# Attention scores as float32r products of split halves, and exponentials of three score tiles at a time

## The chip, the cores and the metric

The kernel runs on one core of one Trainium2 chip (trn2). The metric is the device time of one execution in microseconds. Before the change it is 12858.68 us, the median of three runs (12857.75 to 12866.36).

TensorE is called PE (its weight loads PEld), VectorE DVE, ScalarE ACT, GpSimd POOL. SP is the sync engine, which here only issues DMAs. Every engine takes its own instructions in the order in which the program gives them.

## The reference

The program is one layer of a state-space convolution on 4 images of 64 x 64 tokens with 128 channels, then one layer of attention with a mixture of experts. Only the attention's core is touched. Cut to that:

```python
def _qz_ring(phi):
    c = jnp.cos(phi)
    P = jnp.cumprod(c, axis=-1)
    z0 = jnp.prod(c[..., 1:], axis=-1, keepdims=True)
    return jnp.concatenate([z0, P[..., 1:]], axis=-1)
...
heads = x.reshape(Bs, Ss, H, D)          # 4 images, 4096 tokens, 16 heads of 8
qkv = _qz_ring(heads + rx_theta)
q = jnp.transpose(qkv, (0, 2, 1, 3))
scores = jnp.einsum('bhsd,bhtd->bhst', q, q) / np.sqrt(D)
attn = jax.nn.softmax(scores, axis=-1)
ctx = jnp.einsum('bhst,bhtd->bhsd', attn, q)
```

Queries, keys and values are the same array. For each image and head there are 4096 x 4096 scores, each a sum over only 8 channels. All data are float32.

## The kernel before, in words

**Stages.** A first stage (up to about 2150 us) makes the inputs of the convolution's scans for all images and runs the scans of image 0. Then `opening(0)` (called at line 1470) prepares attention for image 0: `tokens` (line 778) forms the normalised tokens, `heads` and `rings` (lines 867 and 877) form the queries. Then `loop` (line 903) runs once for each of the four images. The calls `beside(i)` (lines 1484 to 1498, and the lambda at 1525) put other work between the rounds of attention: in the loops of images 0 to 2 the scans of the next image (`following`) and, once these are through, the next image's `opening`; also the part `after` attention of the image before (`last`). In the last loop, which runs `by_block`, there are only the parts after attention and the search and gathering of the experts. A closing stage of some 250 us follows. The order on each engine is the order of these calls: the schedule is manual, and `Pace.run(share)` advances a part by `share` of a step for each call.

**Scans.** `Scans.of_image` (line 484) works in 384 steps for an image. One step has an exponential on ACT over 128x1024 (line 530), a product, a scan and a product on DVE (lines 537, 546, 551). In two of every four steps, eight products on PE (line 578) add up the states into `y`.

**Queries and values to memory.** `rings` works on 512 tokens (eight pieces for an image). It forms `ring`, copies it into `v_g` with a one beside each head's 8 values (so that the value product also gives the softmax's denominator), transposes 32x32 blocks (line 893), and SP stores the transposed queries to `d_q` in 16 DMAs (line 899). POOL stores `v_g` to `d_v`.

**The loop.** It loads all queries of the image (`qT`, channels by tokens) and all values (`v`) in 16 DMAs (lines 913 and 914). A turn is one `j` of 4 (the heads 4k + j, k = 0 to 3) and one block of 512 queries. `masked` (line 921) makes a copy of the query block in which only the channels of the heads 4k + j are not zero, so that 32 rows of `qT` times 32 rows of the masked block give the scores of exactly one head. A round is a turn and 128 keys (`kc`, 32 of them); there are 32 x 32 = 1024 rounds in a loop.

- `scores(i)` (line 926): four products of 32 rows, 128 keys by 512 queries, one for each k, into two PSUM tiles of two banks; ACT takes the exponential of each tile (line 939, 128x1024) into SBUF. There are three such PSUM tiles.
- `values(i)` (line 942): four products of 128 keys, 32 columns by 512 queries, that add up in the four 32-partition strips of one PSUM bank, `acc`.
- PE's order is scores(0), scores(1), values(0), scores(2), values(1) and so on, with what `beside` puts behind each `values`.
- At a turn's end `sums` (line 954) copies `acc` on ACT (line 957), and POOL stores the result three rounds later.

PSUM has eight banks: six for scores, one for `acc`, one for all other work.

The profile counts a float32 product as two weight loads and two matmul records.

Of the kernel before, what the change touches and what calls it, by code (L numbers as in the profile page):

```python
# [11 lines left out]
F32 = mybir.dt.float32  # L12
AF = mybir.ActivationFunctionType
ALU = mybir.AluOpType
PSUM = bass.MemoryType.PSUM

P = 128
# [11 lines left out]
B_ROW, C_ROW, X_ROWS = 8, 40, 104  # L29
H, D, FFN = 16, 8, 512  # L30
VW = 9
VPAD = 168
QB = 512
TWO_PI_HI = 6.28125
TWO_PI_LO = 2.0 * math.pi - TWO_PI_HI
ROUND = 1.5 * 2.0**23
# [641 lines left out]
class Attention:  # L678
# [3 lines left out]
    def __init__(self, tc, ctx, w, gate, cols, ident, bank, dram, t1, w_out, sums, sz, x):  # L682
# [20 lines left out]
        self.w1 = const.tile([D, FFN], F32, name="w1")  # L703
        self.w2 = const.tile([P, 4, C], F32, name="w2")

        self.mask = const.tile([P, 4], F32, name="mask")
        self.gate = const.tile([P, E], F32, name="gate")
        self.gate_b = const.tile([2 * E, 1], F32, name="gate_b")
        for k in range(2):
# [1 line left out]
        with tc.tile_pool(name="a_load", bufs=1) as load, tc.tile_pool(  # L711
            name="a_load_ps", bufs=2, space=PSUM
        ) as load_ps:
            raw = load.tile([P, C], F32, name="raw_comb")
            nc.sync.dma_start(out=raw, in_=w["w_comb"])
            ps = load_ps.tile([P, 512], F32, tag="ps", name="ps_comb")
            nc.tensor.transpose(ps[:, :C], raw, ident)
            nc.vector.tensor_copy(self.w_comb, ps[:, :C])
            raw = load.tile([P, 4, D], F32, name="raw_w1")
            nc.sync.dma_start(out=raw, in_=w["w1"].rearrange("(f p) d -> p f d", p=P))  # L720
            ps = load_ps.tile([P, 512], F32, tag="ps", name="ps_w1")
            for f in range(4):
                nc.tensor.transpose(ps[:D, f * P : (f + 1) * P], raw[:, f, :], ident)
            nc.vector.tensor_copy(self.w1, ps[:D])
            raw = load.tile([P, FFN], F32, name="raw_w2")
            nc.sync.dma_start(out=raw, in_=w["w2"])
            ps = load_ps.tile([P, 512], F32, tag="ps", name="ps_w2")
            for f in range(4):
                nc.tensor.transpose(ps[:, f * P : (f + 1) * P], raw[:, f * P : (f + 1) * P], ident)
            nc.vector.tensor_copy(self.w2.rearrange("p f c -> p (f c)"), ps)  # L730
            raw = load.tile([4, 4, 4, D], F32, name="raw_mask")
            nc.gpsimd.memset(raw, 0.0)
            nc.gpsimd.affine_select(
                out=raw, in_=raw, compare_op=ALU.not_equal, fill=1.0,
                base=0, pattern=[[0, 4], [-1, 4], [0, D]], channel_multiplier=1,
            )
            ps = load_ps.tile([P, 512], F32, tag="ps", name="ps_mask")
            nc.tensor.transpose(ps[:, :4], raw.rearrange("j i k d -> j (i k d)"), ident[:4, :4])
            nc.vector.tensor_copy(self.mask, ps[:, :4])
            raw = load.tile([E, C], F32, name="raw_gate")  # L740
            nc.scalar.dma_start(out=raw, in_=gate_w)
            ps = load_ps.tile([P, 512], F32, tag="ps", name="ps_gate")
            nc.tensor.transpose(ps[:, :E], raw, ident[:E, :E])
            nc.vector.tensor_copy(self.gate, ps[:, :E])
# [6 lines left out]
    def begin(self, loop):  # L751

        tc = self.tc
        self.pieces_of(loop, 2)
        self.big = loop.enter_context(tc.tile_pool(name="a_big", bufs=1))
        self.mid = loop.enter_context(tc.tile_pool(name="a_mid", bufs=2))
        self.exps = loop.enter_context(tc.tile_pool(name="a_exps", bufs=4))
        self.ps_s = loop.enter_context(tc.tile_pool(name="a_ps_s", bufs=3, space=PSUM))
        self.ps_o = loop.enter_context(tc.tile_pool(name="a_ps_o", bufs=1, space=PSUM))

    def pieces_of(self, ctx, n, ahead=2, opening=True):
# [4 lines left out]

        self.values = []
        for i in range(2 if opening else 0):
            v_g = self.one.tile([P, 4, VPAD], F32, tag=f"v_g{i}", name=f"v_g{n}_{i}")
            nc.gpsimd.memset(v_g[:, :, H * VW :], 0.0)  # L770
            heads = v_g[:, :, : H * VW].rearrange("p t (h e) -> p t h e", e=VW)
            nc.gpsimd.memset(heads[:, :, :, D], 1.0)
            self.values.append((v_g, heads[:, :, :, :D]))

    def piece(self, shape, tag, name):
        return self.one.tile(shape, F32, tag=tag, bufs=self.n, name=name)
# [74 lines left out]
    def opening(self, b):  # L851
# [1 line left out]


        self.u[b] = self.dram.tile([P, NT, C], F32, name=f"d_un_{b}")
        self.v[b] = self.dram.tile([P, NT, VPAD], F32, name=f"d_v_{b}")
        self.q[b] = self.dram.tile([P, L], F32, name=f"d_q_{b}")
        self.angled[b] = 0
        angles, parts = [], []
        for half in range(2):  # L860
# [16 lines left out]
    def rings(self, b, g, a):  # L877
# [8 lines left out]
            nc.vector.tensor_mul(ring[:, :, d], ring[:, :, d - 1], a[:, :, d])  # L886
        copy(ring[:, :, 0], ring[:, :, D - 1])
        nc.vector.tensor_mul(ring[:, :, 1:], ring[:, :, 1:], a[:, :, 0:1].to_broadcast([P, 4 * H, D - 1]))
        copy(values, ring.rearrange("p (t h) d -> p t h d", h=H))
        nc.gpsimd.dma_start(out=self.v[b][:, cut, :], in_=v_g)  # L890

        blocks = a.rearrange("p (t h) d -> p t (h d)", h=H)
        nc.vector.transpose(blocks.rearrange("p t c -> p (t c)"), ring.rearrange("p h d -> p (h d)"))
        yield
        to = self.q[b][:, g * 512 : (g + 1) * 512].rearrange("(k r) (t i c) -> i k r t c", r=32, i=4, c=32)
        for i in range(4):
            rows = blocks[32 * i : 32 * i + 32].rearrange("r t (k c) -> k r t c", c=32)
            for k in range(4):
                nc.sync.dma_start(out=to[i, k], in_=rows[k])
            if i % 2:  # L900
                yield

    def loop(self, b, beside, by_block=False):
# [3 lines left out]
        self.context[b] = self.dram.tile([P, L], F32, name=f"d_ctx_{b}")  # L907
        self.total[b] = self.dram.tile([L // QB, H, QB], F32, name=f"d_sum_{b}")
        self.whole[b] = 0
        qT = self.big.tile([P, L], F32, tag="qT", name=f"qT_{b}")  # L910
        v = self.big.tile([P, NT, VPAD], F32, tag="v", name=f"v_{b}")
        for g in range(NT // 4):
            nc.sync.dma_start(out=qT[:, g * 512 : (g + 1) * 512], in_=self.q[b][:, g * 512 : (g + 1) * 512])
            nc.sync.dma_start(out=v[:, g * 4 : g * 4 + 4, :], in_=self.v[b][:, g * 4 : g * 4 + 4, :])
        turns = [(j, qb) for j in range(4) for qb in range(L // QB)]
        if by_block:
            turns.sort(key=lambda turn: turn[1])
        rounds = [(j, qb, kc) for j, qb in turns for kc in range(NT)]
        queries, es, accs, later = {}, {}, {}, {}

        def masked(j, qb):
            t = self.mid.tile([P, QB], F32, tag="qm", name=f"qm_{b}_{j}_{qb}")
            nc.vector.tensor_scalar_mul(t, qT[:, qb * QB : (qb + 1) * QB], self.mask[:, j : j + 1])
            queries[j, qb] = t

        def scores(i):

            j, qb, kc = rounds[i]
            es[i] = []
            for pair in range(2):  # L930
                s_ps = self.ps_s.tile([P, 2, QB], F32, tag="s", name=f"s_{b}_{i}_{pair}")
                for k in range(2):
                    at = 32 * (2 * pair + k)
                    nc.tensor.matmul(  # L934
                        s_ps[:, k, :], qT[at : at + 32, kc * P : (kc + 1) * P], queries[j, qb][at : at + 32, :],
                        start=True, stop=True,
                    )
                e = self.exps.tile([P, 2, QB], F32, tag="e", name=f"e_{b}_{i}_{pair}")
                nc.scalar.activation(e, s_ps, AF.Exp, scale=1.0 / math.sqrt(D))  # L939
                es[i].append(e)  # L940

        def values(i):
            j, qb, kc = rounds[i]
            if kc == 0:
                accs[j, qb] = self.ps_o.tile([P, QB], F32, tag="acc", name=f"acc_{b}_{j}_{qb}")
            for k in range(4):
                h = 4 * k + j
                nc.tensor.matmul(  # L948
                    accs[j, qb][32 * k : 32 * k + 32, :], v[:, kc, h * VW : h * VW + 32],
                    es[i][k // 2][:, k % 2, :], start=(kc == 0), stop=(kc == NT - 1),  # L950
                )
            del es[i]

        def sums(j, qb, i):
# [14 lines left out]
                if by_block and j == 3:  # L969
                    self.whole[b] = qb + 1  # L970

            later[i + 3] = store

        masked(0, 0)
        scores(0)
        for i, (j, qb, kc) in enumerate(rounds):
            if i + 1 < len(rounds):
                scores(i + 1)
            values(i)
            if kc == NT - 1:  # L980
                sums(j, qb, i)
            if kc == NT - 12 and i + 12 < len(rounds):
                masked(*rounds[i + 12][:2])
            if i in later:
                later.pop(i)()
            beside(i)
# [443 lines left out]
def tile_kernel(tc, ctx, x, in_proj_w, dirs, out_proj_w, attn, gate, weight1, weight2, out):  # L1430
# [47 lines left out]
    with tc.manual_schedule():  # L1478
        last = Pace()
        n = 3 * NC * NB  # L1480
        for b in range(nb - 1):
            opens = Pace(block.opening(b + 1))

            def beside(i):
# [1 line left out]
                left = 2.1 * (n + 1 - scans.steps.get(b + 1, 0))  # L1486
                block.lag = 2 if left > 0.0 else 0
                scans.did.clear()
                following.run(min(1.3, max(0.5, left / max(1, 860 - i))))
                other = last if not last.done else opens if left == 0.0 else None  # L1490
                if other is None:
                    return
# [22 lines left out]
    with tc.manual_schedule():  # L1515
# [6 lines left out]
            block.after(nb - 1, range(0, 4)), block.after(nb - 1, range(4, 6)), block.after(nb - 1, range(6, blocks - 1)),  # L1522
            experts.search(pairs[-1], blocks - 1),
        )
        block.loop(nb - 1, lambda i: last.run(0.92), True)
        last.rest()
    loop.close()
    with ExitStack() as end:
# [48 lines left out]
```

## Time and profile before

| | |
|---|---|
| median of the runs | 12858.68 us |
| span of the profiled execution, first to last instruction | 12857.0 us (the lowest run is 12857.75) |
| busy: PE, ACT, DVE, POOL | 94%, 84%, 68%, 24% |
| first exponential of the loops of images 0, 1, 2, 3 | 2430, 4982, 7566, 10130 us |
| last exponential of the last loop | 12607.6 us |
| mean granted TensorE clock | 0.964 |

The span in 40 equal slices of 321 us; each digit is the busy share in tenths, PEclk the granted clock of TensorE:

```profile
PE   7888887599999999999999999999999999999996
PEld 3333333122222222333332222332332223333323
DVE  7999998788888777988888779888884211101112
ACT  5677766599999988999999889999998888888882
POOL 2324342232323222223232222332331000000000
PEclk8898988799999999999999999999999999999997
DMA  5666666555555455554554555545553100000005
```

The loops begin in slice 8. From there PE is at nine tenths throughout; ACT is there too until the last scan ends, in slice 31, where DVE falls to almost nothing. The chain of work that ended last lies on PE for 84% of the span, and its lines are these:

```profile
PE s L934 38%; PE acc L948 31%; PE y L578 5%; PE cv L386 3%; PE sp L444 2%; DVE h L546 2%; PE fo L1093 1%; ACT e L939 1%; PE xd L400 1%; PE h L1082 1%; DMA w<-in_L_ffn_weight_dram 1%; DVE dB L537 0%; ACT e L432 0%; ACT ln L437 0%; ACT s L434 0%
```

In the profile's groups of instructions the first number after the bar is the time in which at least one of the group ran, the second the mean duration of one in nanoseconds; then the idle time just ahead of them and what ended it. Matmuls overlap, so the mean duration of one says little about how many fit in a microsecond; the distance from start to start does.

Waits of SP, the DMA queue's own (total in us, times, longest), the largest three and one more that the prediction uses:

```profile
SPq L516 <- PE y L578: 2937.9, 350, 24.7
SPq L567 <- DMA d_du<-x_delta: 2096.1, 236, 23.6
SPq L516 <- DVE h L546: 1306.8, 283, 14.3
...
SPq L1063 <- DMA d_xn<-x1r: 651.5, 8, 103.3
```

### The profile page before, as it was taken

The numbers are of one execution on the slowest core, as the hardware profiler recorded it, in microseconds if no ns is written. First come the engines' busy times: TensorE is split into PE (matmuls) and PEld (weight loads), VectorE is DVE, ScalarE is ACT, GpSimd is POOL, SyncE is SP. The second block draws the span as 40 slices with busy tenths as digits, with TensorE's granted clock in tenths as the row PEclk, the third lists the DMA queues.
The fourth block names the chain that finished last, engine by engine and source line by source line (L and its number), as shares of the span: only waits on it lengthen the run. The fifth ranks groups of instructions, "written<-read, shape, count | busy, mean of one in ns | idle before, by whom it ended". The sixth has DMA issues, their size and how long they took to land.

```text
span 12857.0 us, 215633 instructions
## 1 busy us (share of the span) xinstructions
PE 12118.4 (94%) x85447; PEld 3884.6 (30%) x85447; DVE 8712.2 (68%) x8866; ACT 10742.2 (84%) x10860; POOL 3043.0 (24%) x4007
## 2 busy tenths in 40 slices
PE   7888887599999999999999999999999999999996
PEld 3333333122222222333332222332332223333323
DVE  7999998788888777988888779888884211101112
ACT  5677766599999988999999889999998888888882
POOL 2324342232323222223232222332331000000000
PEclk8898988799999999999999999999999999999997
DMA  5666666555555455554554555545553100000005
GB/s 162 198 188 183 188 183 189 148 134 138 138 135 137 122 147 144 143 130 123 130 134 123 146 140 146 133 121 129 133 122 99 51 18 13 22 17 22 13 21 171
DMA packets 775662, 1553.30 MB, mean 121 GB/s; under 512 B 205198, under 2 KB 392134, under 8 KB 774390
## 3 DMA queue, kind: packets, MB, share of 16 engines
q1 hardware_dynamic: 590686, 1127.02, 34.0%
q0 software_dynamic: 142464, 302.77, 7.7%
q10 hardware_dynamic: 41496, 109.71, 3.3%
q8 instruction: 669, 10.96, 0.4%
q14 instruction: 347, 2.84, 0.1%
HBM read 1230.07 MB, written 308.81 MB: 120 GB/s over the span
## 4 chain that ended last, share of the span: by engine, by line
PE 84%; ACT 5%; DVE 4%; DMA 3%; issue 3%; SPq 0%; ACTq 0%; POOL 0%; DVEq 0%; POOLq 0%
PE s L934 38%; PE acc L948 31%; PE y L578 5%; PE cv L386 3%; PE sp L444 2%; DVE h L546 2%; PE fo L1093 1%; ACT e L939 1%; PE xd L400 1%; PE h L1082 1%; DMA w<-in_L_ffn_weight_dram 1%; DVE dB L537 0%; ACT e L432 0%; ACT ln L437 0%; ACT s L434 0%
## 5 line engine op out<-in xcount | busy, mean ns | idle before, releaser
L939 ACT ACTIVATE e<-s 128x1024 f32<-128x1024 f32 x8192 | 7904.3, 1027 | 1054.3 <-PE s L934 888.8
L934 PE MATMUL s<-qm,qT 32*128 32x512 f32 x32768 | 5438.0, 642 | 107.9 <-DMA v<-d_v 57.4
L948 PE MATMUL acc<-e,v 128*32 128x512 f32 x32768 | 4385.9, 607 | 24.3 <-ACT av L957 21.8
L934 PEld LDWEIGHTS s<-qm,qT 32*128 32x128 f32 x32768 | 1797.4, 183 | 3193.5 <-PE s L934 1410.3
L548 POOL COPY ends<-h 128x1 f32<-128x1 f32 x1152 | 1284.5, 1117 | 2905.0 <-DVE h L546 2895.7
L948 PEld LDWEIGHTS acc<-e,v 128*32 128x32 f32 x32768 | 646.7, 108 | 3159.7 <-issue 3023.3
L546 DVE TENSOR_TENSOR_SCAN h<-delta,ends,du 128x1024 f32<-128x1024 f32 x576 | 1350.7, 2345 | 172.8 <-ACT delta L530 147.6
L546 DVE TENSOR_TENSOR_SCAN h<-dA,ends,dB 128x1024 f32<-128x1024 f32 x576 | 1350.7, 2345 | 120.5 <-ACT dA L530 107.0
L537 DVE TENSOR_TENSOR dB<-du,B 128x1024 f32<-128x1024 f32 x768 | 929.1, 1210 | 693.5 <-PE y L578 590.1
L530 ACT ACTIVATE delta<-delta,A 128x1024 f32<-128x1024 f32 x768 | 887.2, 1155 | 135.1 <-PE y L578 125.7
L530 ACT ACTIVATE dA<-delta,A 128x1024 f32<-128x1024 f32 x768 | 889.0, 1158 | 78.4 <-DMA delta<-d_delta 75.7
L551 DVE TENSOR_TENSOR du<-h,C 128x1024 f32<-128x1024 f32 x768 | 935.2, 1218 | 0.1
L551 DVE TENSOR_TENSOR dB<-h,C 128x1024 f32<-128x1024 f32 x768 | 934.9, 1217 | 0.0
L537 DVE TENSOR_TENSOR du<-du,B 128x1024 f32<-128x1024 f32 x768 | 920.8, 1199 | 0.1
L963 POOL DMA_DIRECT2D d_ctx<-av x512 | 260.1, 517 | 1252.3 <-ACT av L957 1245.9
L386 PE MATMUL cv<-xn,conv 128*128 128x512 f32 x1024 | 488.8, 630 | 32.7 <-DVE xn L321 17.3
L578 PE MATMUL y<-du,sel 128*32 128x256 f32 x6144 | 484.2, 387 | 17.3 <-DVE du L551 17.2
L578 PE MATMUL y<-dB,sel 128*32 128x256 f32 x6144 | 487.1, 389 | 3.4 <-DVE dB L551 3.4
L546 DVE TENSOR_TENSOR_SCAN h<-delta,du 128x1024 f32<-128x1024 f32 x192 | 438.3, 2283 | 50.6 <-ACT delta L530 43.0
L546 DVE TENSOR_TENSOR_SCAN h<-dA,dB 128x1024 f32<-128x1024 f32 x192 | 438.3, 2283 | 31.8 <-ACT dA L530 31.3
L607 POOL DMA_DIRECT2D d_y<-o x512 | 328.8, 673 | 543.3 <-DVE o L594 459.8
L572 POOL DMA_DIRECT2D d_du<-x_delta x272 | 155.2, 571 | 1142.3 <-DVE x_delta L571 1111.9
(263 smaller groups left out, 7642.2 us busy)
## 6 DMA issues: line engine op xcount, KB each, us to landing
delta<-d_delta SPq DMA_DIRECT2D x768, 512.0 KB
du<-d_du SPq DMA_DIRECT2D x576, 512.0 KB
du<-d_du ACTq DMA_DIRECT2D x192, 512.0 KB
d_u<-u POOLq DMA_DIRECT2D x48, 1024.0 KB, 5.9
B<-d_bc SPq DMA_DIRECT2D x96, 512.0 KB
C<-d_bc SPq DMA_DIRECT2D x96, 512.0 KB
d_delta<-r POOLq DMA_DIRECT2D x48, 1024.0 KB, 5.8
us<-d_u SPq DMA_DIRECT2D x384, 128.0 KB
```

Source lines behind the costliest of these rows:

```text
L386: nc.tensor.matmul(ps[:, cut], w["conv"][:, k, m * P : (m + 1) * P], reads(k, g), start=(k == 0), stop=(k == 3))
L530: nc.scalar.activation(tiles["delta", s], t, AF.Exp, scale=A)
L537: nc.vector.tensor_mul(tiles["du", s], du, spread[order, c, "B", j % 2])
L546: nc.vector.tensor_tensor_scan(h, dA, dB, first, ALU.mult, ALU.add)
L548: nc.gpsimd.tensor_copy(ends[order, c][:, at : at + 1], h[:, T - 1 :])
L551: nc.vector.tensor_mul(dB, h, spread[order, c, "C", j % 2])
L578: nc.tensor.matmul(y[32 * g : 32 * g + 32, : T // 4], self.sel[:, j // 2, :], hC[:, 256 * g : 256 * g + 256], start=(j == 0), stop=(j == 3),)
L607: nc.gpsimd.dma_start(out=to.rearrange("p (i j) -> p i j", i=SLICES)[:, :, at : at + n], in_=rows.rearrange("p (i j) -> p i j", i=SLICES),)
L934: nc.tensor.matmul(s_ps[:, k, :], qT[at : at + 32, kc * P : (kc + 1) * P], queries[j, qb][at : at + 32, :], start=True, stop=True,)
L939: nc.scalar.activation(e, s_ps, AF.Exp, scale=1.0 / math.sqrt(D))
L948: nc.tensor.matmul(accs[j, qb][32 * k : 32 * k + 32, :], v[:, kc, h * VW : h * VW + 32], es[i][k // 2][:, k % 2, :], start=(kc == 0), stop ...
L963: nc.gpsimd.dma_start(out=self.context[b][h * D : h * D + D, cut], in_=av[32 * k : 32 * k + D, :])
```

## The change

A query is split into two parts whose sum is exact: `high` keeps the upper 20 bits of the float32 word (mask 0xFFFFF000), and the rest is the difference. Both go to memory. For a head the key tile holds on its 32 rows the 8 channels four times, as high, low, high, low; the query tile as high, low, low, high. One product over 32 rows then adds high x high, low x low, high x low and low x high, which is the whole product. The mask over the heads is gone, since a tile now holds only one head's channels in each strip of 32 rows. Both operands are declared float32r.

- `rings`: 32 stores on SP where there were 16, of `ring` (which now holds the high part) and of the transposed tile; two more DVE operations on 128x512; four copies into `v_g` where there was one.
- `loop`: nothing is held for the whole image. `fetch` loads the keys and values of one j and 512 tokens, in 8 + 1 DMAs on SP, three such chunks ahead, into ten buffers; a chunk that is still held for the same j isn't loaded again. In images 0 to 2 that makes 32 loads; in the last loop, where j changes with every turn, 256. `masked` now loads a query tile in 12 DMAs, twelve keys' tiles ahead of its turn.
- The units (turn, kc, k) are cut into tiles of three, over the bounds of rounds and turns: 1366 tiles in a loop. A score tile has three PSUM banks, and there are two such tiles where there were three of two banks. One exponential takes 128x1536. The value products of a tile follow as before; at a turn's end those of the next turn wait for the next tile.
- The shares of `Pace` are set to three quarters, as there are 1366 calls of `beside` in place of 1024.

The core of the diff:

```diff
-        blocks = a.rearrange("p (t h) d -> p t (h d)", h=H)
-        nc.vector.transpose(blocks.rearrange("p t c -> p (t c)"), ring.rearrange("p h d -> p (h d)"))
+        blocks, high = (t.rearrange("p h d -> p (h d)") for t in (a, ring))
+        nc.vector.transpose(blocks, high)
+        nc.vector.tensor_single_scalar(high.bitcast(bits), blocks.bitcast(bits), HIGH, ALU.bitwise_and)
+        nc.vector.tensor_sub(blocks, blocks, high)
...
+            for x, t in enumerate((high, blocks)):
...
+                for k in range(4):
+                    nc.sync.dma_start(out=to[i, k], in_=rows[k])
...
-        for g in range(NT // 4):
-            nc.sync.dma_start(out=qT[:, g * 512 : (g + 1) * 512], in_=self.q[b][:, g * 512 : (g + 1) * 512])
-            nc.sync.dma_start(out=v[:, g * 4 : g * 4 + 4, :], in_=self.v[b][:, g * 4 : g * 4 + 4, :])
+        units = [(at, kc, k) for at in range(len(turns)) for kc in range(NT) for k in range(4)]
+        tiles = [units[i : i + WIDE] for i in range(0, len(units), WIDE)]
...
+        def halves(to, j, cut, order):
+            src = self.q[b][:, :, cut].rearrange("x (k j d) t -> j k x d t", j=4, d=D)[j]
+            for k in range(4):
+                at = 32 * k
+                for part in order:
+                    n = D * (part.stop - part.start)
+                    nc.sync.dma_start(out=to[at : at + n], in_=src[k, part])
+                    at += n
+        def fetch(at):
...
+            if held.get(g) != j:
+                held[g] = j
+                keys[g] = self.big.tile([P, QB], F32, tag="keys", bufs=10, name=f"key_{b}_{at}")
+                halves(keys[g], j, slice(g * QB, (g + 1) * QB), (slice(0, 2), slice(0, 2)))
+                weights[g] = self.big.tile([P, 4, VJ], F32, tag="values", bufs=10, name=f"val_{b}_{at}")
+                nc.sync.dma_start(out=weights[g], in_=self.v[b][:, j, g * 4 : g * 4 + 4, :])
...
         def masked(j, qb):
             t = self.mid.tile([P, QB], F32, tag="qm", name=f"qm_{b}_{j}_{qb}")
-            nc.vector.tensor_scalar_mul(t, qT[:, qb * QB : (qb + 1) * QB], self.mask[:, j : j + 1])
+            halves(t, j, slice(qb * QB, (qb + 1) * QB), (slice(0, 2), slice(1, 2), slice(0, 1)))
+        def ahead(at, kc):
+            if kc % 4 == 0:
+                fetch(at * 8 + kc // 4 + 3)
+            if kc == NT - 12 and at + 1 < len(turns):
+                masked(*turns[at + 1])
         def scores(i):
+            s_ps = self.ps_s.tile([P, WIDE, QB], F32, tag="s", name=f"s_{b}_{i}")
+            for n, (at, kc, k) in enumerate(tiles[i]):
+                rows, cut = slice(32 * k, 32 * k + 32), slice(kc % 4 * P, kc % 4 * P + P)
+                nc.tensor.matmul(
+                    s_ps[:, n, :], keys[f"{at * 8 + kc // 4}"][rows, cut].bitcast(F32R),
+                    queries[turns[at]][rows, :].bitcast(F32R), start=True, stop=True,
+                )
...
+            nc.scalar.activation(es[i][:, :n, :], s_ps[:, :n, :], AF.Exp, scale=1.0 / math.sqrt(D))
...
-                following.run(min(1.3, max(0.5, left / max(1, 860 - i))))
+                following.run(min(1.0, max(0.4, left / max(1, 1146 - i))))
...
-        block.loop(nb - 1, lambda i: last.run(0.92), True)
+        block.loop(nb - 1, lambda i: last.run(0.69), True)
```

## The prediction

> **What bounds it now.** I read the page's groups first, then busy time by stretch for the four attention loops (cut where each image's first exponential starts), then the order of time inside a loop. Three groups carry the loops:
>
> ```profile
> L939 ACT ACTIVATE e<-s 128x1024 f32<-128x1024 f32 x8192 | 7904.3, 1027 | 1054.3 <-PE s L934 888.8
> L934 PE MATMUL s<-qm,qT 32*128 32x512 f32 x32768 | 5438.0, 642 | 107.9 <-DMA v<-d_v 57.4
> L948 PE MATMUL acc<-e,v 128*32 128x512 f32 x32768 | 4385.9, 607 | 24.3 <-ACT av L957 21.8
> ```
>
> The groups kept apart by shape price a 512-wide PSUM read on ACT:
>
> ```profile
> L957 ACT COPY av<-acc 128x512 f32<-128x512 f32 x128 | 76.6, 598 | 6.2 <-PE acc L948 5.4 <-DMA d_v<-v_g 0.8
> ```
>
> The stretches (us; PE, weight loads, DVE, ACT, POOL) show PE full in all four loops, and ACT nearly so in the first three, where the next image's scans run too:
>
> ```profile
> 2430.00:4982.00 2552.00, 2537.17 (x19810) 731.84 (x19810) 2095.74 (x1770) 2388.19 (x2500) 653.58 (x906) 1.00 0.53 135
> 4982.00:7566.00 2584.00, 2563.12 (x20052) 773.25 (x20048) 2116.05 (x2143) 2381.63 (x2474) 740.73 (x955) 0.99 0.52 134
> 7566.00:10130.00 2564.00, 2539.95 (x19762) 761.82 (x19760) 1924.11 (x1996) 2342.35 (x2433) 671.13 (x896) 0.99 0.47 122
> 10130.00:12608.00 2478.00, 2458.54 (x17626) 748.89 (x17624) 373.71 (x973) 2016.20 (x2109) 173.94 (x308) 0.99 0.07 21
> ```
>
> Order of time where nothing else runs:
>
> ```profile
> 11202.34 1.14 PE L934 MATMUL s<-qm,qT 32*128 32x512 f32 x8
> ...
> 11203.41 1.07 PE L948 MATMUL acc<-e,v 128*32 128x512 f32 x8
> 11203.58 4.00 ACT L939 ACTIVATE e<-s 128x1024 f32<-128x1024 f32 x4 [0.36 <-PE s L934]
> ...
> 11207.94 1.94 ACT L939 ACTIVATE e<-s 128x1024 f32<-128x1024 f32 x2 [0.36 <-PE s L934]
> ```
>
> PE alone, where a scan's sums come in:
>
> ```profile
> 7801.53 1.14 PE L934 MATMUL s<-qm,qT 32*128 32x512 f32 x8
> 7802.60 1.07 PE L948 MATMUL acc<-e,v 128*32 128x512 f32 x8
> 7803.48 0.61 PE L578 MATMUL y<-dB,sel 128*32 128x256 f32 x8
> 7803.91 0.61 PE L578 MATMUL y<-du,sel 128*32 128x256 f32 x8
> 7804.46 1.14 PE L934 MATMUL s<-qm,qT 32*128 32x512 f32 x8
> ```
>
> Starts matter here, not durations. A block of 8 records (4 products of 2 records, the four side by side in 32-row or 32-column strips of the array) holds PE for 1.07 us when it is scores (7801.53 to 7802.60). A value block holds it 0.88 when a sum of the same shape follows, and 1.00 when scores follow (the next score start after 11203.41 comes at 11204.41): a **change of shape costs 0.12**, as 0.43 against 0.55 for the sum blocks says too. A sum block is two passes of 256 columns in 0.43, so a pass streams 0.84 ns a column, 0.43 for 512. Scores are then 2 x 0.43 + 0.21 (shape 0.12, exposed weights 0.09), values 2 x 0.43 + 0.14. PE needs 2.07 for a round of four heads; quiet rounds take (11207.94 - 11203.58) / 2 = 2.18. Two exponentials end in 1.94 with 1.02 for one, so ACT starts one each 0.92: 1.84 a round.
>
> **The change, by parts.** 4096 head-units a loop make 1365.3 tiles of three.
>
> *Exponentials.* ACT's slope is (1.02 - 0.598) / 512 = 0.83 ns an element, so 1536 elements last 1.02 + 0.43 = 1.45 and follow each other each 0.92 + 0.43 = 1.35: 1843 a loop against 2048 x 0.92 = 1884. That alone is 41 us of ACT.
>
> *Scores.* One record per product where there were two. No row shows a float32r product. Bounds: the record streams at 0.43 like any recorded pass (the 128-column transposes, one record each, start 0.109 apart, the same rate), or at half. I take **half, 0.215**: the two records now make the four products of two halves each, two per 0.43, and the change lays these four on 32 rows instead (hi, lo, hi, lo against hi, lo, lo, hi), so a record carries one. Score block: 0.21 + 0.215 = 0.43, or 0.64.
>
> *Values.* Untouched in form, but now three products per block, not four. They run side by side, so a block of three still costs two passes, 1.00: 1365 x 1.00 against 1024 x 1.00, **341 us more PE a loop**, shape changes included. Scores fall from 1024 x 1.07 = 1096 to 587. PE's net is 168 a loop.
>
> *The wait that becomes last.* Only two score tiles are left, so S(i+2) needs exp(i) done; PE's order puts V(i) ahead of it, which needs exp(i) as well. The chain exp(i), V(i), S(i+2), exp(i+2) costs 1.45 + 0.05 (from that exponential's end to the weight load it frees, single records) + 1.00 + from score start to exponential. Today that is 11202.34 to 11203.58, 1.24; less one pass 0.81, less another half pass 0.60. **Sum 3.10 for two tiles, 1.55 a tile**: above ACT's 1.35 and PE's 1.43. Quiet loop: 1365.3 x 1.55 = 2116.
>
> *Scans beside it* (413, 384, 343 exponentials at L530 in loops 0 to 2). One delays the next ACT start by 1.04. With one each third tile, the gap with it is 1.35 + 1.04 = 2.39, the other two gaps together are one chain, 3.10: 5.49 against 4.65, so 0.84 each; far apart, 1.04 - (3.10 - 2.70) = 0.64. They come each 3.3 to 3.6 tiles; I take 0.84. The sum blocks (0.86 of PE, in half of the steps) fall into the same gap and are free; uncovered they would cost 0.86 less PE's 0.24 slack. For comparison, today (2552 - 1024 x 2.18 - 18) / 413 = 0.73. Other PE work, block by block from the records of the lines that are neither scores, values nor sums, is 18, 80, 80 and 166 us; in the last loop 2478 - 2232 - 166 = 80 is unexplained and I keep it.
>
> Loop 0: 2116 + 347 + 18 = 2481 (-71). Loop 1: 2116 + 323 + 80 = 2519 (-65). Loop 2: 2116 + 288 + 80 = 2484 (-80). Loop 3: 2116 + 166 + 80 = 2362 (-116). Together **-332**.
>
> *SP's queue.* Each of the 32 ring pieces issues 32 query stores, not 16. The last 64 stores of the first image went out back to back, 2386.20 to 2417.02, 0.48 each, with the loop waiting: +31 for twice as many, and the first half's ring buffers are now held by their stores too (+14 taken, 0 to 60). In loops 0 to 2 the same bursts double, 31 to 62 us per half image, and the second half's loads for the token pieces stand behind them on SP, with PE in order behind those: +25 a loop taken, 0 to 60. Fetches are 9 issues a chunk, query tiles 12 a turn: 288 + 384 a loop, 2304 + 384 in the last, at 0.32 to 0.43 each. A chunk's 3.2 us fits 5.3 tiles (8 us) and it is issued three chunks (some 25 us) ahead, so I cost it at nothing; if that cover went, each late chunk would stop PE. At each loop's start the first tile waits for 20 such issues instead of two loads: +13 in all. Together **+133**.
>
> *DVE.* 128 masks (0.475) go; each ring piece gains a mask and a subtraction (about 0.5 + 0.69), 38 us in all, off the path with DVE at 82% in loops 0 to 2. ACT's four short copies for one are nothing.
>
> The Trainium skill speaks against the change: TensorEngine Tiling (Array Packing), Key Properties, says that changing the tiling mode drains TensorE. The 0.12 agrees, and 683 more changes a loop, two for each of 341 more blocks, are within the 341 us above. Its FP8 and Floating Point Precision page, TensorE Precision Notes, has true FP32 as four passes and a reduced form that truncates to FP22; by that, estimated, the score stream is a quarter of 0.86, 0.215, and the sum stays; by the transposes' row it is 0.43, the first rival.
>
> **Sum.** -332 + 133 = -199. The profiled span is 12857.0; the median of the runs, 12858.7, is 1.7 above it, and I add the difference to that: **12660**.
>
> **Rivals.**
> 1. *The score record streams at 0.43* (slower than before). The chain is 3.31, a tile 1.655: +143 a loop, less 0.1 per scan exponential, +460 in all: **13120**. For it: every single-record row runs at that rate. Against: the count of products. It decides from a stream of about 0.31 on, where the 199 are gone. 13%.
> 2. *Fetches late on SP.* For it: SP already stood up to 103 us at L1063 for a store to land, in the last loop, and its queue is in order. 256 chunks there late by 2 us each are +512: **13170**; half of that, 12900. Against: that wait ends with work emitted before it, so SP runs ahead of PE, not behind. 10%.
> 3. *The chain does not bind*, only PE's 1.43 a tile: 0.12 x 5461 = 655 less, partly given back to the scans: **12150**. PE would have to start S(i+2) before V(i), and its records show no such thing. 4%.
> 4. *It does not do what it says*, the products still take two records: 0.64 more per chain than 0.60, 0.32 a tile: **14400**. 3%.
>
> **Chances.** The forecast, 70%, spreads from 12450 (scan exponentials at 0.64, -230) to 12860 (all SP terms at their upper ends, +210). The range 12450 to 13060 leaves out most of rival 1, parts of 2, and 3 and 4. Faster by over 0.2% 0.69 (66 of the forecast's 70 and most of rival 3), within 0.2% 0.07, slower 0.24; 0.2%, 26 us, is about what a measurement here can tell from no change.
>
> **What would show it.** Right: score records halved to 16384 and shorter by 0.37 or more; value blocks still 1.00 from start to the next score start; in quiet stretches exponentials of 1.45 starting 1.55 apart with some 0.2 of ACT idle; PE below 95% in the loops; the last loop gaining most. Wrong: score blocks at 0.64 (rival 1); score weight loads ended by a DMA of key, or SP waits in front of the fetches (rival 2); exponentials back to back in the quiet stretches (rival 3). What would break the sum with the mechanism intact is the bursts of query stores: gaps of tens of us where the rings are written, near 2400 and late in loops 0 to 2.

## The result, and the profile after

The changed kernel takes 13070.88 us, the median of four runs (13063.4 to 13073.58); the kernel before took 12860.14 beside it (12857.75 to 12866.36, four runs). The ratio is 1.0162 [1.0147, 1.0176]: 211 us slower, 411 above the forecast of 12660 and 11 above the upper end of the range.

The profile's groups, as shown for before (busy, mean ns of one, idle time ahead and its releaser), and one group that before had with 75.7 us of waiting for its input:

```profile
L968 ACT ACTIVATE e<-s 128x1536 f32<-128x1536 f32 x5464 | 7788.9, 1449 | 1108.3 <-PE s L962 996.9
L977 PE MATMUL acc<-e,val 128*32 128x512 f32 x32768 | 5934.1, 616 | 1111.3 <-ACT e L968 1024.3
L962 PE MATMUL s<-qm,key 32*128 32x512 f32 x16384 | 2842.2, 500 | 100.3 <-DMA key<-d_q 99.8
...
L535 ACT ACTIVATE dA<-delta,A 128x1024 f32<-128x1024 f32 x768 | 877.6, 1143 | 346.0 <-DMA delta<-d_delta 325.0
```

The score records are halved, and the mean of one is shorter by 0.14; the value products now wait 1024 us for exponentials. The last line is the surprise: the scans' exponentials, which the change does not touch, wait 325 us for a load of `delta`.

The four loops, cut as before (length; busy PE, weight loads, DVE, ACT, POOL; granted clock, DMA share, GB/s):

```profile
2489.90:5184.80 2694.90, 2247.52 (x15744) 607.72 (x15744) 2110.16 (x1789) 2354.87 (x1823) 652.19 (x908) 0.96 0.54 137
5184.80:7855.80 2671.00, 2315.89 (x15952) 651.65 (x15952) 2108.99 (x2150) 2340.03 (x1790) 757.46 (x958) 0.96 0.53 136
7855.80:10443.00 2587.20, 2284.24 (x15635) 638.97 (x15635) 1900.38 (x1987) 2301.10 (x1746) 697.33 (x884) 0.97 0.49 128
10443.00:12819.00 2376.00, 2223.82 (x13534) 614.11 (x13532) 361.89 (x941) 1996.44 (x1428) 173.78 (x307) 0.99 0.21 64
```

The last loop gained 102 us; the first three lost 143, 87 and 23. They are the ones that have scans of the next image beside attention. The first exponential comes at 2490 in place of 2430.

Order of time where little else runs, in the last loop:

```profile
11498.74 2.87 ACT L968 ACTIVATE e<-s 128x1536 f32<-128x1536 f32 x2 [0.99 <-PE s L962]
...
11500.25 1.06 PE L977 MATMUL acc<-e,val 128*32 128x512 f32 x6 [0.20 <-ACT e L968]
...
11501.24 0.50 PE L962 MATMUL s<-qm,key 32*128 32x512 f32 x3
...
11501.67 1.06 PE L977 MATMUL acc<-e,val 128*32 128x512 f32 x6
11501.84 2.88 ACT L968 ACTIVATE e<-s 128x1536 f32<-128x1536 f32 x2 [0.23 <-PE s L962]
```

A score block holds PE for 0.43 (11501.24 to 11501.67), a value block of three for 0.99 (11500.25 to 11501.24), and two tiles take 3.10 (11498.74 to 11501.84), with 0.23 of ACT idle. The scores start 0.60 ahead of their exponential (11501.24 to 11501.84); before it was 1.24.

**Where the time went** in the first three loops is the order on SP. Late in each loop the next image's rings are written. SP (start, duration and count of DMA issues in a row), from the end of the last burst of loop 0:

```profile
5052.71 1.85 SPq L901 DMA_DIRECT2D d_q<-ring  x4
5054.61 1.85 SPq L901 DMA_DIRECT2D d_q<-ang  x4
5056.50 0.52 SPq L502 DMA_DIRECT2D B<-d_bc  x1
...
5057.92 0.59 SPq L521 DMA_DIRECT2D delta<-d_delta  x1
```

and what ACT did then:

```profile
5066.52 1.15 ACT L535 ACTIVATE dA<-delta,A 128x1024 f32<-128x1024 f32 x1 [40.01 <-DMA delta<-d_delta]
```

One piece's 32 stores take SP about 15 us, at 0.46 each, and here 96 of them, those of three pieces, stand between two loads of `delta` (issued at 5004.41 and 5057.92). The loads of the next scan step stand behind the stores in the same queue, ACT stands at the exponential that needs the load, attention's exponentials stand behind that one on ACT, and PE behind those: 41 us without a matmul.

The token loads `y` of the next image's `opening` stand behind the stores as well. Late in loop 1, SP and then PE:

```profile
7520.99 1.85 SPq L901 DMA_DIRECT2D d_q<-ang  x4
...
7525.22 1.45 SPq L790 DMA_DIRECT2D y<-d_y  x3
```

```profile
7536.02 0.80 PE L803 MATMUL out<-w_out,y 128*128 128x128 f32 x2 [38.29 <-DVE y L795]
```

Here PE itself stands in order at a product of the opening, 38 us, with attention behind it.

The other place is the start of a new `j`, where `fetch` loads three chunks close together. SP:

```profile
4428.77 5.02 SPq L929 DMA_DIRECT2D key<-d_q  x8
...
4435.60 0.54 SPq L521 DMA_DIRECT2D delta<-d_delta  x1
```

and ACT:

```profile
4447.46 1.15 ACT L535 ACTIVATE dA<-delta,A 128x1024 f32<-128x1024 f32 x1 [6.04 <-DMA delta<-d_delta]
```

A chunk costs SP 5.0 us (13.8 where it waits in between, at 4440.40), and the scan's load comes behind it. ACT goes on 11.9 us after that load was issued, against 8.6 after the burst above (5057.92 to 5066.52), so part of this wait may be slower landing beside the key loads. The trace can be summed: of each distance of over 3 us between the start of one matmul and the next I take what exceeds 0.7. The table has the loops' lengths and these sums in us, in the last 14% of a loop (rings) and before (the rest), in loops 0, 1 and 2; then the experiments.

| kernel | us | loops 0 to 3 | waits late | waits elsewhere |
|---|---|---|---|---|
| before | 12860 | 2552 2584 2564 2478 | 8, 8, 7 | 0, 6, 9 |
| after | 13071 | 2695 2671 2587 2376 | 85, 87, 47 | 65, 51, 46 |
| e1, low halves' stores on POOL | 12900 | 2635 2621 2566 2376 | 38, 39, 18 | 50, 59, 54 |
| e10, all stores on POOL | 13000 | 2658 2647 2571 2373 | 63, 69, 30 | 48, 55, 49 |
| e2, key loads on POOL | 12947 | 2649 2636 2543 2378 | 90, 98, 47 | 27, 21, 15 |
| e9, e1 and e2 together | 12762 | 2591 2586 2512 2374 | 44, 49, 16 | 12, 19, 20 |
| e3, scores two ahead | 12625 | 2575 2590 2501 2211 | 93, 92, 49 | 83, 77, 62 |
| e4, rounds of four | 12332 | 2513 2509 2448 2127 | 68, 69, 47 | 63, 75, 67 |
| e5, tiles of three alone | 14978 | 3055 3107 3098 3032 | 10, 10, 7 | 4, 0, 8 |
| e8, e3 with e1 and e2 | 12255 | 2444 2489 2405 2218 | 55, 64, 19 | 32, 46, 44 |
| e7, e4 with e1 and e2 | 11972 | 2405 2403 2356 2119 | 26, 24, 18 | 22, 31, 40 |

### The profile page after: what moved, and what is told of

Read it like the earlier page. It is cut to its first block, busy times and chain, and to the rows that moved or that the text cites. A ratio compares the mean times of both kernels' runs of the same rounds, so it can differ in the third digit from the quotient of the medians.

```text
span 13071.9 us, 185113 instructions
## 1 busy us (share of the span) xinstructions
PE 11087.8 (85%) x69062; PEld 3380.6 (26%) x69062; DVE 8699.6 (67%) x8873; ACT 10608.7 (81%) x8156; POOL 3098.8 (24%) x4017
## 5 line engine op out<-in xcount | busy, mean ns | idle before, releaser
L968 ACT ACTIVATE e<-s 128x1536 f32<-128x1536 f32 x5464 | 7788.9, 1449 | 1108.3 <-PE s L962 996.9
L977 PE MATMUL acc<-e,val 128*32 128x512 f32 x32768 | 5934.1, 616 | 1111.3 <-ACT e L968 1024.3
L962 PE MATMUL s<-qm,key 32*128 32x512 f32 x16384 | 2842.2, 500 | 100.3 <-DMA key<-d_q 99.8
L962 PEld LDWEIGHTS s<-qm,key 32*128 32x128 f32 x16384 | 1056.2, 183 | 4204.8 <-issue 2684.9
L553 POOL COPY ends<-h 128x1 f32<-128x1 f32 x1152 | 1324.5, 1152 | 3019.8 <-DVE h L551 3015.1
L977 PEld LDWEIGHTS acc<-e,val 128*32 128x32 f32 x32768 | 840.9, 109 | 2713.1 <-ACT e L968 2250.4
L583 PE MATMUL y<-dB,sel 128*32 128x256 f32 x6144 | 835.9, 394 | 15.2 <-DVE zT L1106 6.1
L583 PE MATMUL y<-du,sel 128*32 128x256 f32 x6144 | 740.2, 390 | 16.7 <-DVE du L556 16.6
```

The lines of the kernel that those rows point to most:

```text
L553: nc.gpsimd.tensor_copy(ends[order, c][:, at : at + 1], h[:, T - 1 :])
L583: nc.tensor.matmul(y[32 * g : 32 * g + 32, : T // 4], self.sel[:, j // 2, :], hC[:, 256 * g : 256 * g + 256], start=(j == 0), stop=(j == 3),)
L962: nc.tensor.matmul(s_ps[:, n, :], keys[f"{at * 8 + kc // 4}"][rows, cut].bitcast(F32R), queries[turns[at]][rows, :].bitcast(F32R), start=T ...
L968: nc.scalar.activation(es[i][:, :n, :], s_ps[:, :n, :], AF.Exp, scale=1.0 / math.sqrt(D))
L977: nc.tensor.matmul(accs[turn][32 * k : 32 * k + 32, :], weights[f"{at * 8 + kc // 4}"][:, kc % 4, k * VW : k * VW + 32], e, start=(kc == 0 ...
```

## The experiments

The theory after the result: the prediction's chain of exponential, values and scores is right, and what it missed is SP's queue, in two places that can be eased one by one. Its rivals are other causes of the same waits (buffers of the rings held by their stores), a dearer chain, and a float32r product that is not worth what I gave it. The kernels of e7 and e9 were run four times, the others once; the four runs of e9 spread over 24 us.

**e1: half of the stores leave SP.**

```diff
-                    nc.sync.dma_start(out=to[i, k], in_=rows[k])
+                    (nc.sync, nc.gpsimd)[x].dma_start(out=to[i, k], in_=rows[k])
```

> The changed kernel, with the stores of the low halves (line 901) issued by POOL, so that SP has 16 stores for a ring piece again and not 32. Theory 1 (SP's queue is the bound in bursts: scan and token loads stand behind the doubled stores): the waits of PE over 3 us late in loops 0 to 2 (85, 87, 47 us) fall to 30 or less each and the first exponential comes at about 2445 instead of 2490, in all some 12870. Theory 2 (two score tiles leave the scans no slack, the queue is innocent): within 30 us of 13071. Theory 3 (not the queue but the ring buffers, held until their stores land): POOL's stores land no sooner, the late waits stay above 60 each, 13000 or more.

12899.6, one run, where the kernel before took 12863.4 on the same chip; 171 less than the change. The late waits fell by more than half, though in loops 0 and 1 not to the 30 or less that was expected; the last loop, which writes no rings, did not move, and the first exponential came at 2448.8, 41 earlier. SP at the same place as above:

```profile
4947.17 8.06 SPq L901 DMA_DIRECT2D d_q<-ring  x16
4955.27 1.59 SPq L502 DMA_DIRECT2D B<-d_bc  x1
...
4957.60 0.55 SPq L521 DMA_DIRECT2D delta<-d_delta  x1
```

16 stores of 0.50 in a row, 8 us, and ACT's wait behind them is 10.9. The number of stores is unchanged, so their landing and the buffers they hold can't be the main cause: with these the late waits were to stay above 60. The queue they stand in is.

**e10: all stores leave SP.** What the remaining 38, 39 and 18 us are.

```diff
-                    nc.sync.dma_start(out=to[i, k], in_=rows[k])
+                    nc.gpsimd.dma_start(out=to[i, k], in_=rows[k])
```

> All 32 query stores of a ring piece on POOL, none on SP; key loads stay on SP. Asks what the PE gaps over 3 us are that remained late in the loops (38, 39 and 18 us) when half of the stores had left SP. If they are the other half of the bursts, late gaps fall to 10 us or less in each of the loops 0 to 2, as long as the loop of the kernel before with its 16 stores had (8, 8, 7), and the time is near 12820. If they are something else in the work on the rings (DVE, the transposes, POOL's own stores), they stay near 38, 39 and 18, and the time stays near 12900 or rises where POOL's queue is now the late one.

12999.8: worse than e1, and not the 12820 of the first possibility. The late waits are 63, 69 and 30, and the second possibility's last clause is what happened: POOL is now the late queue. A store costs POOL 0.54. This is POOL late in loop 0:

```profile
4849.12 2.17 POOL L901 DMA_DIRECT2D d_q<-ring  x4
...
4853.57 0.56 POOL L577 DMA_DIRECT2D d_du<-x_delta  x1
```

and SP's waits in the 90 us around it (total, times, longest):

```profile
SPq L572 <- DMA d_du<-x_delta: 61.8, 2, 45.5
```

POOL's own store `d_du` stood behind the ring stores, and SP stood 45.5 us for that store, with the token loads behind it; PE then stood 36.1 at L803. The burst is not cured by another queue: it moves to who shares it. How much of e1's remaining 38, 39 and 18 is SP's half and how much POOL's, this run does not tell, since each queue carries loads that the other waits for.

**e2: the key loads of loops 0 to 2 leave SP.**

```diff
-def halves(to, j, cut, order):
+def halves(to, j, cut, order, by):
...
-                    nc.sync.dma_start(out=to[at : at + n], in_=src[k, part])
+                    by.dma_start(out=to[at : at + n], in_=src[k, part])
...
-halves(keys[g], ...)
+halves(keys[g], ..., nc.sync if by_block else nc.gpsimd)
```

> The changed kernel, with the eight key loads of a chunk issued by POOL in loops 0 to 2 (the last loop as it was). Theory 1 (SP's bursts): the waits over 3 us away from the loops' ends (63, 53, 47 us, in the first turns of each j) fall below 20 each, in all 110 us less, some 12960; the last loop stays at 2376. Theory 2 (no slack for the scans): they stay, 13071 within 30. If POOL's own work (the copies of scan ends) suffers, the time rises and DVE's scans show waits for POOL.

12947.1, 124 less than the change. The waits outside the rings fell from 65, 51 and 46 to 27, 21 and 15; the late ones did not fall. The same bytes are loaded, so the larger part is the place in the queue and not the transfer. Below 20 each was expected; what the remaining 27 and 21 are, this run does not tell.

**e9: both, and nothing else.** Does SP's queue alone decide the sign?

> The change with both loads of SP's queue eased and nothing else: POOL issues the stores of the low halves and the key loads of the loops of images 0 to 2; order, tiles and float32r as in the change. Theory 1 (SP's queue alone puts the change on the wrong side): the two gains measured one by one add up, 13071 - 171 - 124 = 12776, and anything from 12700 to 12830 supports it; the loops of images 0 to 2 are near 2585, 2585, 2520, the last one unchanged near 2376. Rival (the two stand in for each other, the same stalls counted twice, or the work moved to POOL now binds): 12860 or more, no better than the kernel before.

12762.49 (12743.88 to 12767.4, four runs) against 12855.62: ratio 0.9923 [0.9906, 0.994]. The two gains add up to 295 and together give 308. So the change as it stands is on the wrong side because of SP's queue; with the same order on PE and ACT it is 0.8% faster. Loop 0 is 104 shorter than in the change, at the same 15744 matmul records; the last one, where nothing was moved, is 2 shorter.

**e3: scores two tiles ahead**, so that S(i+2) no longer stands behind V(i). The test of the chain.

```diff
         scores(0)
+        scores(1)
...
-            if i + 1 < len(tiles):
-                scores(i + 1)
+            if i + 2 < len(tiles):
+                scores(i + 2)
```

> The changed kernel, with PE's order turned: S(i+2) ahead of V(i), so that the chain exp(i), S(i+2), exp(i+2) no longer holds V. If the chain of 3.10 us for two tiles is the bound of the quiet stretches: PE's 1.43 takes its place, exponentials start 1.43 apart, the last loop falls from 2376 to about 2212, loops 0 to 2 by 50 to 150 each, in all 12600 to 12800. If the chain is not the bound (ACT or the wait for slots in general): the last loop stays within 20 of 2376.

12624.8, 446 less than the change; the last loop is 2211. The quiet stretch:

```profile
11500.73 5.72 ACT L968 ACTIVATE e<-s 128x1536 f32<-128x1536 f32 x4 [0.96 <-PE s L962]
...
11501.98 1.06 PE L977 MATMUL acc<-e,val 128*32 128x512 f32 x6
...
11503.40 1.06 PE L977 MATMUL acc<-e,val 128*32 128x512 f32 x6
```

Four exponentials follow each other without a gap, and a tile takes 1.42, PE's 0.43 + 0.99, where the change has 1.55. The chain was the bound, as the prediction had it, and here PE takes its place. The waits of SP's queue are all still there, even larger: that a shorter loop leaves them less cover would explain it, but no run shows it.

**e4: the float32r half alone**: rounds of four heads, exponentials of two score tiles (128x1024) and three buffers, as before, with the shares of `Pace` of before; fetches and stores as in the change.

```diff
-        tiles = [units[i : i + WIDE] for i in range(0, len(units), WIDE)]
+        tiles = [units[i : i + 4] for i in range(0, len(units), 4)]
...
+            for pair in range(2):
+                s_ps = self.ps_s.tile([P, 2, QB], F32, tag="s", ...)
...
+                nc.scalar.activation(e, s_ps, AF.Exp, scale=1.0 / math.sqrt(D))
```

> The float32r half of the change alone: rounds of four heads, three score tiles of two banks and exponentials of 128x1024 as before the change, scores in one float32r record on the split halves with their loads and stores. If the tiles of three are what costs (a value block of three takes as long as one of four, two score tiles make the chain): PE needs 0.43 + 1.00 = 1.43 a round, ACT 2 x 0.92 = 1.84 becomes the bound, quiet rounds of 1.84 to 1.90, the last loop about 1950, loops 0 to 2 about 2450 (SP's bursts stay), in all about 12100. If float32r brings little and SP's queue is nearly the whole of the loss: 12860 or more.

12332.2: the direction is right, the size is not. The quiet stretch (PEld is the weight load):

```profile
11201.13 0.14 PEld L979 LDWEIGHTS acc<-e,val 128*32 128x32 f32 x4 [0.25 <-issue]
11201.13 1.46 PE L979 MATMUL acc<-e,val 128*32 128x512 f32 x8
11201.54 0.14 PEld L979 LDWEIGHTS acc<-e,val 128*32 128x32 f32 x4 [0.27 <-ACT e L969]
...
11202.96 0.14 PEld L979 LDWEIGHTS acc<-e,val 128*32 128x32 f32 x4 [0.24 <-issue]
```

A round takes 1.83 (11201.13 to 11202.96), which is ACT's two exponentials. The round is as expected, the last loop is not (2127, where I had about 1950). I had given the value block its 1.00 of before; it takes 1.40 (scores follow at 11202.53), since its second pair waits for the round's second exponential and is not side by side with the first. So PE is full at 1.83 too, and the other work of the last loop, which I had let fit into PE's slack, comes on top: 1024 x 1.83 and the prediction's 166 and 80 of other work are 2120.

**e5: the tiles of three alone**, on the kernel before: float32 products, resident queries and values. (`av` has one buffer there, for space.)

> The other half of the change alone: the kernel before, with its masked float32 queries, its resident keys and values and its 16 stores a ring piece, but in tiles of three with exponentials of 128x1536 and two score tiles (its copy of a turn's result has one buffer, not two, for room). If the chain through two tiles is what such tiles cost: 1.45 + 0.05 + 1.00 + 1.25 (two recorded passes) = 3.75 for two tiles, a quiet loop of 2560, the last loop 2740 to 2820, loops 0 to 2 about 2800, in all 13800 to 14000. If the tiles of three are harmless by themselves and the loss of the whole change is the queue's alone: 12860 or less.

14977.9, worse than the expected 13800 to 14000. I had let the chain set the pace, at 1.875 a tile; PE itself is longer:

```profile
12500.75 1.06 PE L948 MATMUL acc<-e,v 128*32 128x512 f32 x6
...
12501.73 1.13 PE L932 MATMUL s<-qm,qT 32*128 32x512 f32 x6
12502.80 1.06 PE L948 MATMUL acc<-e,v 128*32 128x512 f32 x6
```

A tile is 0.98 of values and 1.07 of scores, 2.05: blocks of three cost what blocks of four cost, in a third more of them. It says two things of the change: tiles of three are a loss by themselves, and without the fetches and the doubled stores the long waits are not there (10 us at most late in a loop).

**e8: e3 with both loads of SP eased.**

> Tiles of three kept, with S(i+2) ahead of V(i) and both relieved queues. By the same sum 12625 - 296 = 12329, the last loop at 2211. It tells whether the wide exponential, with both of its costs mended, beats rounds of four (12036): by PE, 1.43 a tile of three heads against ACT's 1.84 a round of four, it should not.

12254.8, 370 less than e3 where 296 was expected. It stays above e7, the next run, as expected: the wide exponential does not beat rounds of four.

**e7: e4 with both loads of SP eased.**

> Rounds of four with float32r scores, and both relieved queues: the low halves' stores and, in loops 0 to 2, the key loads on POOL. If what the two moves take away is the queue's and independent of the order on PE, their 172 and 124 us come off again: 12332 - 296 = 12036, with 12000 to 12100 as the band. If the stalls only move to POOL or to ACT's bound: 12250 or more.

11971.87 (11961.22 to 11983.66, four runs) against 12860.94: ratio 0.9305 [0.9289, 0.932]. That is 360 less than e4 and 28 below the expected band. It beats both kernels: the exact halves without the tiles of three, and with SP's queue eased.

## Why the prediction was wrong, point by point

**What held.** The score record streams at half: the block is 0.43 as predicted, against 1.07 before, and the way from score start to exponential lost 0.64, which is one pass of 0.43 and half of another. (The sign that the prediction gave, records "shorter by 0.37 or more", was ill chosen: the mean of a record fell by 0.14 only. Records overlap, and the starts carry the price.) The Trainium skill's FP8 and Floating Point Precision page (TensorE Precision Notes) has true float32 as four passes; the estimate from it, a stream of 0.215 per block, agrees with the 0.64. The value block of three costs 0.99 (predicted 1.00); the exponential 1.45; the chain 3.10 for two tiles, to the hundredth; e3 shows that it is the bound. The last loop was to be 2362, of which 80 were a remainder carried over unexplained, and is 2376. Rivals 1, 3 and 4 are out by these rows. The opening's stores were to cost 45 (31 and 14) and cost 54: their last burst, 2407.66 to 2470.65, is 32.2 longer than before and starts 21.5 later. The first loads of queries and keys make the other 6 of the 60 by which the first exponential came later.

**The step that failed** is the part on SP's queue. It costed the fetches "at nothing", because it asked only whether the *fetched* tile comes in time. It does: of the 99.8 us in which score products waited for keys, 94.5 are one wait in the opening and 3.1 lie after 5170. What is late is what stands *behind* the fetches on SP, the scans' loads, and behind them two engines in order, ACT and then PE. For the store bursts it had "+25 a loop taken, 0 to 60", for the token loads behind them. That path is there, and near its size: PE's late waits at L803 are 21, 46 and 38 us in the three loops, where before had none of over 3 us. What it left out are the scans' loads behind the same stores: PE's late waits for attention's exponentials are 62, 40 and 9. With those outside the rings, the waits for exponentials are 254 us, and 213 of them fall where ACT stood at a scan exponential for `delta`.

The three loops were to take 7484 and took 7953; for the stores and the loop starts the forecast had 75 and 13 on top. Of the 469 us, 381 are waits of over 3 us (219 late, 162 elsewhere; before had 38 in all). The late ones of loops 0 and 1 are 77 and 79 above those of before, beyond the upper bound of 60. With 15 from the opening, 14 from the last loop and 3 from the closing stage the profiled run's miss is 469 - 88 + 32 = 413. Prices were low as well: a key load costs SP 0.576, where I had 0.32 to 0.43 from other rows, so that a chunk takes 5.0 in place of 3.2.

Two slips changed little. The upper ends of the SP terms, as stated, add 151 and not 210 to the forecast; and the copies into `v_g` are ACT's only for the first image (32 of 128), DVE's for the others.

**Rival 2** named SP, at 10%, but in the last loop, with its 256 chunks, and for PE's own tiles. There nothing came of it: 11 us of long waits. The loops with only 32 chunks paid, since they have the scans beside them. The closing sentence, which put the bursts "near 2400 and late in loops 0 to 2", had the place and not the size.

**The other 88 us** of the 469, in no wait of over 3 us, are 64, 14 and 10 in the three loops. The sum with 0.84 for a scan exponential thus comes out within 14 us in loops 1 and 2, but no run shows the 0.84 by itself. A part that the prediction did not have is the granted clock after a long wait. PE after the 41 us:

```profile
5069.06 1.93 PE L977 MATMUL acc<-e,val 128*32 128x512 f32 x6 [41.00 <-ACT e L968]
5070.92 0.80 PE L962 MATMUL s<-qm,key 32*128 32x512 f32 x3
5071.65 1.93 PE L977 MATMUL acc<-e,val 128*32 128x512 f32 x6
```

and the stretches before and after it (the clock is the third column from the end):

```profile
5015.00:5025.00 10.00, 9.53 (x73) 2.58 (x75) 1.89 (x7) 9.30 (x7) 0.10 (x1) 1.00 0.27 48
5069.00:5071.00 2.00, 1.94 (x9) 0.28 (x9) 2.00 (x3) 1.35 (x2) 0.00 (x0) 0.50 1.03 229
...
5073.00:5075.00 2.00, 2.00 (x9) 0.48 (x9) 2.00 (x3) 0.86 (x2) 1.25 (x1) 0.50 1.03 231
5075.00:5080.00 5.00, 5.00 (x27) 1.01 (x21) 1.35 (x2) 3.87 (x4) 0.97 (x1) 0.72 0.43 119
```

For some 8 us a tile takes 2.59 (1.86 + 0.73) in place of 1.55. Value records of over 0.8 us, which mark such tiles, are 749 in the three loops and were 112 before: 637 more. A tile has six, so these are 106 tiles, at most 110 us at 1.04 each, or 45, 44 and 21 by loop. The loops leave only 64, 14 and 10 beside the waits, so part of this must lie beside other waits, or the 0.84 was too high; no run here separates it, and I leave the share open. The Trainium skill's TensorE: Matmul & The Clock Gate (Part 1, What's actually happening) states this: half clock after about 3.4 us of idleness, full clock after as much sustained work. The trace agrees on the halving; the return took longer here, from 5069 to about 5078 (the clock is 0.72 over 5075 to 5080), with PE busy throughout.

**Open:** the 64 us of loop 0; the clock's share; and what is left of the late waits in e9 (44, 49 and 16). Of these 22, 17 and 9 are waits for attention's exponentials and 13, 23 and 8 waits at L803, as in the change; which of the two queues they are due to, no run separates.

## What to carry to other kernels

When a change adds DMA issues to an in-order queue, price them by who stands behind them, not by whether their own data come in time; the victims here were scan loads and token loads that the diff never mentions, and through them ACT and PE. Spread a burst over two queues rather than move it whole: half of it on each cost 171 us less, all of it on the other only 71 less. Test the halves of a combined change by themselves: here one half alone is worth 528 us, and the other, put on top of it, costs 739.

## What the runs showed of the hardware

- Three products side by side hold PE as long as four (0.98 to 1.00 against 1.00), and two pairs that come apart take 1.40.
- A DMA issue costs SP 0.576 us for a key tile's part, 0.43 at the median for a query tile's part or a ring store and 0.34 for a value chunk; on POOL 0.54 to 0.59 for the same stores and key parts. In a burst they add up without overlap.
- After 41 us without work TensorE had a granted clock of 0.50 for nearly 9 us more; each of the changed kernel's shorter waits (3 to 8 us, loops 0 to 2) was followed by value records of over 0.8 us as well, for 3.5 us or longer.
